# One TensorE-heavy tail and one batch boundary rearranged: a product pair in two sums, three groups parked in SBUF, two sigmoids one block earlier

## The chip, the cores and the metric

The kernel runs on one core of a Trainium2 chip. The metric is device microseconds of one execution; the kernel before takes 492.13 us (median of 3 runs, 490.97 to 493.98). All times below are microseconds from the start of the span of one profiled execution, unless a unit is given.

## The reference, cut to what matters

The input `x` and the side input `k` (used as key and as value) are (4, 1024, 1024): four batches, 1024 rows in time, 1024 channels. A bidirectional decaying scan runs along time, its result is gated by a sigmoid of `x`, and a feed-forward product with a binarized weight follows, with the input added.

```python
ek  = exp(min(k, 30));  ekv = ek * k
nf, df = scan forward  of (ekv, ek):  a = a*decay + ekv_t ; b = b*decay + ek_t
nb, db = scan backward of (ekv, ek)
euk = exp(min(u + k, 30))
num = nf + nb - ekv + euk * k
den = df + db - ek + euk
mix = sigmoid(x) * (num / max(den, 1e-8)) * (0.8 + 0.2*tf)      # tf: one number per batch
bw  = where(weight >= 0, 1, -1) * mean(|weight|, axis=1)        # (out, in)
out = x + einsum('bsi,oi->bso', mix, bw) + bias
```

## The kernel before, in words

**Steps.** Work is cut into blocks of 128 channels by 1024 time steps: 4 batches of 8 blocks, so 32 steps, `g` = 0 to 31. The order of instructions on every engine is written out by hand (`tc.manual_schedule()`); each engine runs its own list in order and waits on semaphores for the others. There is no planner: what stands earlier in the list of an engine blocks what stands later.

**One step on each engine.** SP (the DMA queue of SyncE) loads `k_rows` and `sg_rows` two steps ahead. TensorE (PE) transposes `k_rows` to `kT` (L266) and `sg_rows` to `sgT` (L272), both in PSUM. ScalarE (ACT) takes exponentials of `kT` (L278, L284), a logarithm and an exponential that together are a reciprocal (L404, L411), tiny edge factors for the backward scans (L372, `edge_num` and `edge_den`) and the rounded high part of the gated result (L433, `act_hi`). VectorE (DVE) has eight instructions of 128x1024 in each step: four scans (L366, L379) and four others (L350, L356, L389, L423). GpSimd (POOL) has the floor (L396), a clamp (L346), three products (L416, L419, L428) and the low part of the gated result (L438, `lo_part`), which is stored in `gated` beside the high part. A block that is scanned in step g has its high and low part ready in step g + 2. Sigmoids of two blocks are taken together in every odd step (L111), between two loads of ScalarE's function table (L111 and L94).

**Products of batches 0 to 2.** For each batch there are 16 groups (two halves of time by eight blocks of output channels). A group is a sum of 16 products in PSUM: eight blocks by high and low part (`pe_product`, L449). ACT scales it into SBUF (`z`, L461), PE turns it four times 128x128 (L469), ACT copies it to `staged` (L557), and after two groups SP stores the pair (L135). The lists `parts[g]` and `late[g]` say which pieces of which groups run in which place of a step; `fresh`, `ready`, `scaled`, `leaving` are the stages on the way out. The input `x` is added afterwards in DRAM: `add_x` (L140, POOL's queue) adds 1 MB of `x` into 256 rows of `out` in each call, one call in every second step from step 16 on, and the four calls of batch 2 after step 31.

**The last batch** needs no turning: `pe_wide_product` (L517) uses the gated block as weights, so rows of time come out. There are 8 row groups n by two halves of the columns (`part`), again 16 products each. VectorE multiplies each by `alpha_rows` (L539), adds it to `x_rows[n]` (L541) and adds `bias_rows` (L531); SP stores.

**PSUM** has three buffers in the pool `ps_o`, handed out in turn to `po`, `turned` and `wide` tiles: a new tile waits until the tile three allocations earlier has been read out. `ps_k` and `ps_g` hold `kT` and `sgT` and are used for wide groups at the end.

Of the kernel before, what the change touches and what calls it, by code (L numbers as in the profile page):

```python
# [21 lines left out]
def kernel(  # L22
# [28 lines left out]
    P = 128  # L51
# [8 lines left out]
    const = ctx.enter_context(tc.tile_pool(name="const", bufs=1))  # L60
    gpool = ctx.enter_context(tc.tile_pool(name="gpool", bufs=3 * NC))
    rows = ctx.enter_context(tc.tile_pool(name="rows", bufs=2))
    gate_rows = ctx.enter_context(tc.tile_pool(name="gate_rows", bufs=3))
    resid = ctx.enter_context(tc.tile_pool(name="resid", bufs=2))
# [40 lines left out]
    def load_gate(g):  # L105
        t = gate_rows.tile([P, NT, P], F32, tag="sg_rows", name=f"sg_rows_{g}")
        nc.sync.dma_start(out=t, in_=column_block(x, g))
        sg_rows[g] = t
# [5 lines left out]
    def group(q):  # L114
        b, r = divmod(q, NH * NC)
        h, oc = divmod(r, NC)
        return b, h, oc
# [16 lines left out]
    def store(q):  # L134
        nc.sync.dma_start(out=pair_of(out, q), in_=x_pairs[q])  # L135

    def add_x(b, n):

        rows = slice(2 * n * P, 2 * (n + 1) * P)
        nc.gpsimd.dma_start(  # L140
            out=out[b, rows, :], in_=x[b, rows, :], accum_op=ALU.add, max_dma_last_dim=8192
        )
# [284 lines left out]
    def gated_product(g, ts=slice(0, T), engine=nc.gpsimd):  # L427
        engine.tensor_mul(nums[g][:, ts], dens[g][:, ts], nums[g][:, ts])  # L428
# [12 lines left out]


    def pe_product(q, blocks):
        b, h, oc = group(q)
        if q not in prods:
            prods[q] = ps_o.tile([P, H], F32, tag="po", name=f"po_{q}")
        for cc in blocks:
            for i in range(2):
                nc.tensor.matmul(  # L449
                    prods[q],  # L450
                    wT[:, cc, oc * P : (oc + 1) * P],
                    gated[b, cc, h][:, i, :],
                    start=(cc == 0 and i == 0),
                    stop=(cc == NC - 1 and i == 1),
                )

    def act_scale(q):
        b, h, oc = group(q)
        one = slice(oc, oc + 1)
        z = work.tile([P, H], F32, tag="z", name=f"z_{q}")  # L460
        nc.scalar.activation(  # L461
            z, prods[q], AF.Identity, scale=out_scale[:, b, one], bias=bias_col[:, one]
        )
        z_sb[q] = z
# [47 lines left out]

    def pe_wide_columns(t, n, cols, blocks):
        h, s = divmod(n, PER)
        for cc in blocks:
            for i in range(2):
                nc.tensor.matmul(  # L517
                    t,
                    gated[last, cc, h][:, i, s * P : (s + 1) * P],
                    wT[:, cc, cols],  # L520
                    start=(cc == 0 and i == 0),
                    stop=(cc == NC - 1 and i == 1),
                )
# [5 lines left out]

    def dve_add_bias(n):  # L530
        nc.vector.tensor_add(x_rows[n], x_rows[n], bias_rows)  # L531

    def columns(part):
        return slice(part * H, (part + 1) * H)

    def leave_columns(ps, n, cols):
        width = cols.stop - cols.start
        t = work.tile([P, width], F32, tag="z", name=f"wide_{n}_{cols.start}")
        nc.vector.tensor_mul(t, ps, alpha_rows[:, cols])  # L539
        xs = x_rows[n][:, cols]  # L540
        nc.vector.tensor_add(xs, xs, t)  # L541

    def leave_wide(n, part):
        leave_columns(wide[n, part], n, columns(part))

    def store_wide(n, part):
        rows = out[last, n * P : (n + 1) * P, columns(part)]
        nc.sync.dma_start(out=rows, in_=x_rows[n][:, columns(part)])

    def finish_wide(n):  # L550
        dve_add_bias(n)
        nc.sync.dma_start(out=out[last, n * P : (n + 1) * P, :], in_=x_rows[n])

    def act_leave(q):
        if q % 2 == 0:
            stage(q)
        nc.scalar.copy(x_res[q], turned[q])  # L557
        if q % 2 == 1:
            store(q - 1)

# [11 lines left out]
    def pieces(qs):  # L572
        return [(q, part) for q in qs for part in (front, back)]

    def fill(g, part, items):
        for i, piece in enumerate(items):
            ahead, at = divmod(part + i, 5)
            parts[g + ahead][at].append(piece)
# [9 lines left out]
    for i in range(3):  # L588
        parts[g - 1][2 + i].append((q + i, front))
        parts[g][1 + i].append((q + i, range(NC // 2, NC - 1)))  # L590
        late[g + 1].append((q + i, range(NC - 1, NC)))
    for part, piece in enumerate(pieces((q + 3, q + 4))):
        parts[g + 1][1 + part].append(piece)
    fill(g + 2, 0, pieces(range(q + 5, q + groups)))


    adds = {g: [] for g in range(steps + 1)}
    for b in range(B - 1):
        for n in range(NT // 2):
            adds[min((b + 2) * NC + 2 * n, steps)].append((b, n))  # L600

    with tc.manual_schedule():
# [33 lines left out]
        def product(pieces):  # L636
            for q, blocks in pieces:
                pe_product(q, blocks)
                if blocks[-1] == NC - 1:
                    fresh.append(q)  # L640

# [4 lines left out]
        def scale():  # L646
            while ready:
                scaled.append(ready.pop(0))
                act_scale(scaled[-1])

# [9 lines left out]
        for g in range(steps):  # L660
            b, cc = divmod(g, NC)
            final = g == steps - 1
            if g + 2 < steps:
                load_k(g + 2)
                load_gate(g + 2)
            else:
                load_x_rows(g + 2 - steps, rows, "k_rows")
                load_x_rows(g + 4 - steps, gate_rows, "sg_rows")
# [8 lines left out]
            for i in adds[g]:  # L677
                add_x(*i)
            if final:
                done()  # L680
# [58 lines left out]
            scale()  # L739
            if final:  # L740
                pe_wide_product(0, 1, range(NC - 2))
            product(parts[g][2])
            if g == steps - 2:
                pe_wide_product(1, 0, range(NC - 3))
            if g > 0:
                dve_newton_gate(g - 1)
            if g > 0 and not final:
                gated_product(g - 1)
            gates = (g + 1, g + 2) if cc % 2 == 1 and not final else ()
            if g == 0:  # L750
                gates = (0, 1)
            for i in gates:
                act_gate(i)
            if gates:
                log_exp_tables()
            pe_transpose_gate(g)
            product(parts[g][3])
            turn()
            if parts[g][4]:
                done()  # L760
            product(parts[g][4])
            if g == steps - 2:
                pe_wide_product(1, 1, range(NC - 3))
            if final:
                gate = num_pool.tile([P, T], F32, tag="num", name="gate_of_last")
                nc.scalar.copy(gate, sg_ps[g])
                sg_ps[g] = gate
            leave()
# [10 lines left out]
        load_x_rows(4, gate_rows, "sg_rows")  # L779
        for i in adds[steps]:  # L780
            add_x(*i)

        for i in ((2, 1), (3, 0), (3, 1)):
            pe_wide_product(*i, range(NC - 2))

# [5 lines left out]
        for ts in halves:  # L791
            act_reciprocal(g, ts)
        gated_product(g - 1, engine=nc.vector)
        for h in range(NH):
            act_hi(g - 1, h)
        for h, ts in enumerate(halves):
# [6 lines left out]
            lo_part(g, h, nc.vector)  # L803
        for n in range(5, NT):
            load_x_rows(n, eu_pool, "eu")

        waiting = [(n, part) for n in range(4) for part in range(2)]
        for i in waiting:
            pe_wide_product(*i, range(NC - 2, NC))
        for i in waiting:  # L810
            leave_wide(*i)
        biased = iter((0, 4, 1, 5, 2, 6, 3))
        for n in range(4, NT - 1):
            for part in range(2):
                pe_wide_product(n, part, range(NC))
                if n != 5:
                    leave_wide(n, part)
                    finish_wide(next(biased))

            for part in range(2 if n == 5 else 0):  # L820
                leave_wide(n, part)
                finish_wide(next(biased))
        dve_add_bias(NT - 1)
        finish_wide(next(biased))
        n = NT - 1
        for cols, pool, tag in (
            (slice(0, H), ps_o, "po"),
            (slice(H, 3 * H // 2), ps_o, "po"),
            (slice(3 * H // 2, C), ps_k, "kT"),
        ):  # L830
            bank_of = pool.tile([P, cols.stop - cols.start], F32, tag=tag, name=f"last_{cols.start}")
            pe_wide_columns(bank_of, n, cols, range(NC))
            leave_columns(bank_of, n, cols)
            nc.sync.dma_start(
                out=out[last, n * P : (n + 1) * P, cols], in_=x_rows[n][:, cols]
            )

# [29 lines left out]
```

## Time and profile before

| | |
|---|---|
| time, median of 3 | 492.13 us (490.97 to 493.98) |
| the profiled execution | 494.9 us, of it 493.1 us span |
| DVE busy | 475.5 us, 96% of the span |
| POOL / PE / ACT busy | 402.2 / 369.1 / 336.8 us |
| granted TensorE clock, mean | 0.875 |
| one step on DVE | 13.5 us (num L379 at 380.00, 393.50, 407.10) |
| last scan of DVE | starts at 439.78 |
| last 54 us | PE busy without a gap from 434.76 to 488.93 |

A line of the profile names the engine, the source line, the operation, output and input tiles and the count. In a timeline the columns are start, duration, what ran, and in brackets the idle time of that engine just before it and what ended it. The chain of work that ended last is followed back from the last instruction. Busy time of an engine is no bound by itself: DVE is 96% busy over the span, but in the last 54 us PE has no gap and DVE has.

### The profile page before, as it was taken

The numbers are of one execution on the slowest core, as the hardware profiler recorded it, in microseconds if no ns is written. First come the engines' busy times: TensorE is split into PE (matmuls) and PEld (weight loads), VectorE is DVE, ScalarE is ACT, GpSimd is POOL, SyncE is SP. The second block draws the span as 40 slices with busy tenths as digits, with TensorE's granted clock in tenths as the row PEclk, the third lists the DMA queues.
The fourth block names the chain that finished last, engine by engine and source line by source line (L and its number), as shares of the span: only waits on it lengthen the run. The fifth ranks groups of instructions, "written<-read, shape, count | busy, mean of one in ns | idle before, by whom it ended". The sixth has DMA issues, their size and how long they took to land.

```text
span 493.1 us, 5241 instructions
## 1 busy us (share of the span) xinstructions
PE 369.1 (75%) x1813; PEld 298.4 (61%) x1813; DVE 475.5 (96%) x331; ACT 336.8 (68%) x466; POOL 402.2 (82%) x276
## 2 busy tenths in 40 slices
PE   3334443334677788778999999978699998989996
PEld 2333333233555666666777777756587777868885
DVE  6999999999999999999999999999989999998967
ACT  4795968779585868669696878784597978724000
POOL 3389999999999999999999999999979999991000
PEclk9955555556899999979999999979799999989999
DMA  8846556663546655549976996799389499899945
GB/s 226 231 127 164 142 138 167 170 170 85 144 113 170 159 150 143 142 107 233 255 161 155 266 234 168 147 240 226 75 136 292 99 270 256 193 244 221 255 183 198
DMA packets 89762, 89.49 MB, mean 181 GB/s; under 512 B 2660, under 2 KB 80776, under 8 KB 88200
## 3 DMA queue, kind: packets, MB, share of 16 engines
q1 hardware_dynamic: 83320, 59.78, 40.5%
q0 software_dynamic: 6400, 29.37, 31.5%
q8 instruction: 14, 0.23, 0.2%
q14 instruction: 12, 0.10, 0.1%
q10 hardware_dynamic: 16, 0.00, 0.0%
HBM read 55.59 MB, written 29.36 MB: 172 GB/s over the span
## 4 chain that ended last, share of the span: by engine, by line
DVE 60%; PE 21%; ACT 7%; POOL 6%; issue 4%; DMA 0%; SPq 0%; POOLq 0%; DVEq 0%; ACTq 0%
DVE den L379 11%; DVE num L366 10%; DVE den L366 10%; DVE num L379 9%; PE wide L517 8%; PE po L449 7%; DVE den L389 5%; DVE den L423 5%; DVE num L350 5%; DVE euk L356 3%; POOL den L416 2%; PE last L517 1%; POOL gated L438 1%; PE kT L266 1%; ACT eu L404 1%
## 5 line engine op out<-in xcount | busy, mean ns | idle before, releaser
L449 PE MATMUL po<-gated,wT 128*128 128x512 f32 x768 | 204.7, 413 | 5.4 <-POOL gated L438 3.7
L449 PEld LDWEIGHTS po<-gated,wT 128*128 128x128 f32 x768 | 142.4, 194 | 35.4 <-POOL gated L438 4.0
L266 PE MATMUL kT<-ident,k_rows 128*128 128x128 f32 x248 | 42.6, 328 | 61.6 <-issue 39.0
L438 POOL TENSOR_TENSOR gated<-num,gated 128x512 fp32r<-128x512 f32 x60 | 75.6, 1280 | 5.2 <-ACT gated L433 3.0
L379 DVE TENSOR_TENSOR_SCAN num<-bank,edge_num,num 128x1024 f32<-128x1024 f32 x32 | 74.9, 2339 | 2.7 <-ACT edge_num L372 2.7
L266 PEld LDWEIGHTS kT<-ident,k_rows 128*128 128x128 f32 x248 | 34.1, 168 | 71.0 <-issue 47.3
L379 DVE TENSOR_TENSOR_SCAN den<-bank,edge_den,den 128x1024 f32<-128x1024 f32 x32 | 74.9, 2341 | 1.0 <-ACT edge_den L372 1.0
L416 POOL TENSOR_TENSOR den<-den,eu 128x1024 f32<-128x1024 f32 x31 | 73.7, 2377 | 2.4 <-ACT eu L411 2.4
L419 POOL TENSOR_TENSOR num<-num,eu 128x1024 f32<-128x1024 f32 x31 | 73.7, 2379 | 1.0 <-DMA num<-euk 1.0
L428 POOL TENSOR_TENSOR num<-den,num 128x1024 f32<-128x1024 f32 x30 | 71.9, 2395 | 2.8 <-DVE den L423 0.5
L272 PE MATMUL sgT<-ident,sg_rows 128*128 128x128 f32 x256 | 42.9, 322 | 41.3 <-DVE den L423 36.0
L366 DVE TENSOR_TENSOR_SCAN den<-bank,den 128x1024 f32<-128x1024 f32 x32 | 72.3, 2259 | 0.0
L366 DVE TENSOR_TENSOR_SCAN num<-bank,num 128x1024 f32<-128x1024 f32 x31 | 70.6, 2278 | 0.0
L272 PEld LDWEIGHTS sgT<-ident,sg_rows 128*128 128x128 f32 x256 | 35.1, 166 | 52.7 <-DVE den L423 25.2
L396 POOL TENSOR_SCALAR den<-den,floor 128x1024 f32<-128x1024 f32 x31 | 36.5, 1178 | 21.1 <-DVE den L389 15.7
L433 ACT CAST gated<-num 128x512 fp32r<-128x512 f32 x64 | 36.5, 619 | 22.6 <-POOL num L428 18.2
L557 ACT COPY staged<-turned 128x512 f32<-128x512 f32 x48 | 27.7, 578 | 33.1 <-PE turned L469 33.1
L404 ACT ACTIVATE eu<-den,gain 128x1024 f32<-128x1024 f32 (+1 forms) x33 | 36.9, 1121 | 17.6 <-POOL den L396 17.6
L517 PE MATMUL wide<-wT,gated 128*128 128x512 f32 x192 | 46.6, 400 | 2.1 <-POOL gated L438 2.1
L517 PEld LDWEIGHTS wide<-wT,gated 128*128 128x128 f32 x192 | 36.7, 192 | 10.5 <-POOL gated L438 2.5
L389 DVE SCALAR_TENSOR_TENSOR den<-eu,top,den 128x1024 f32<-128x1024 f32 (+1 forms) x33 | 41.7, 1265 | 0.0
L356 DVE SCALAR_TENSOR_TENSOR euk<-eu,top,kT 128x1024 f32<-128x1024 f32 x31 | 38.8, 1250 | 0.0
(91 smaller groups left out, 579.9 us busy)
## 6 DMA issues: line engine op xcount, KB each, us to landing
sg_rows<-in_x_dram SPq DMA_DIRECT2D x32, 512.0 KB, 5.5
num<-euk POOLq DMA_DIRECT2D x32, 512.0 KB, 5.9
k_rows<-in_fside_BxSxS_dram SPq DMA_DIRECT2D x31, 512.0 KB, 4.9
out_dram<-staged SPq DMA_DIRECT2D x24, 512.0 KB, 4.1
out_dram<-in_x_dram POOLq DMA_DIRECT2D x12, 1024.0 KB, 11.9
w_rows<-in_L_ffn_weight_dram SPq DMA_DIRECT2D x8, 512.0 KB, 5.0
x_rows<-in_x_dram SPq DMA_DIRECT2D x8, 512.0 KB, 12.5
out_dram<-x_rows SPq DMA_DIRECT2D x7, 512.0 KB, 2.6
```

The costliest lines, as they stand in the source:

```text
L266: nc.tensor.transpose(kT[:, s * P : (s + 1) * P], k_rows[g][:, s, :], ident)
L272: nc.tensor.transpose(t[:, s * P : (s + 1) * P], sg_rows[g][:, s, :], ident)
L356: nc.vector.scalar_tensor_tensor(euk, eus[g], top[:, b, cc : cc + 1], k_ps[g], ALU.min, ALU.mult)
L366: nc.vector.tensor_tensor_scan(t, decay_row(g), t, 0.0, ALU.mult, ALU.add)
L379: nc.vector.tensor_tensor_scan(back, decay_row(g), back, inits[g, which], ALU.mult, ALU.add)
L389: nc.vector.scalar_tensor_tensor(dens[g][:, ts], eus[g][:, ts], top[:, b, cc : cc + 1], dens[g][:, ts], ALU.min, ALU.add,)
L416: engine.tensor_mul(dens[g][:, ts], dens[g][:, ts], eus[g][:, ts])
L419: engine.tensor_mul(nums[g][:, ts], nums[g][:, ts], eus[g][:, ts])
L428: engine.tensor_mul(nums[g][:, ts], dens[g][:, ts], nums[g][:, ts])
L438: engine.tensor_sub(t[:, 1, :], nums[g][:, h * H : (h + 1) * H], t[:, 0, :].bitcast(F32))
L449: nc.tensor.matmul(prods[q], wT[:, cc, oc * P : (oc + 1) * P], gated[b, cc, h][:, i, :], start=(cc == 0 and i == 0), stop=(cc == NC - 1 an ...
L517: nc.tensor.matmul(t, gated[last, cc, h][:, i, s * P : (s + 1) * P], wT[:, cc, cols], start=(cc == 0 and i == 0), stop=(cc == NC - 1 and i ...
```

## The change

It has five parts.

1. **Two groups of batch 2 in two sums.** `split` names groups 4 and 5 of batch 2, a pair. Their products over blocks 0 to 5 run in step 23, leave through `z` (a plain copy with scale, without bias), turn, `staged` and a store; their blocks 6 and 7 run in step 25 as a sum of their own, and that pair is added into `out` by an accumulating DMA of 512 KB on POOL's queue (`add_sum`, first step after it without an `add_x`; the built order has it in step 27). Groups 0 to 2 of batch 2, whose first halves ran in step 23, now run in step 24.
2. **Sigmoids of blocks 26 and 27 in step 24** in place of step 25, with their loads earlier (`gate_loads`), `gate_rows` with four buffers and `gpool` with one less.
3. **Three groups of the last batch over five blocks.** In step 30 PE sums groups (6,0), (6,1) and (5,0) over blocks 0 to 4; ACT copies them to SBUF (`act_partial`). The groups (1,0) and (1,1) move behind them. At the end PE has only blocks 5 to 7 of these three groups left. POOL multiplies the parked sums by `alpha_rows` and adds them, with the bias, to `x_rows[6]` and half of `x_rows[5]`.
4. **The end in another order**: row groups 4, 7, 5, 6. Group 4 leaves through an ACT copy and two POOL operations for each half, and is stored from ACT's queue. VectorE multiplies in place in PSUM. Of the four `add_x` of batch 2, one moves to step 29, one stays right behind step 31, two stand behind POOL's work on `x_rows[6]` and `x_rows[5]`. `x_rows` are loaded in the order 5, 7, 6.
5. **The copy of the last gate** stands behind the reciprocals of the last block, and (0,1) behind it; `scale()` holds at most two scaled groups.

The diff, cut to its core:

```diff
-    gpool = ctx.enter_context(tc.tile_pool(name="gpool", bufs=3 * NC))
+    gpool = ctx.enter_context(tc.tile_pool(name="gpool", bufs=3 * NC - 1))
-    gate_rows = ctx.enter_context(tc.tile_pool(name="gate_rows", bufs=3))
+    gate_rows = ctx.enter_context(tc.tile_pool(name="gate_rows", bufs=4))
...
+    split = (2 * NH * NC + 4, 2 * NH * NC + 5)
+    before, after = range(NC - 2), range(NC - 2, NC)
     def pe_product(q, blocks):
+        ends = (0, NC - 1)
+        if q in split:
+            ends = (blocks[0], blocks[-1])
...
     def act_scale(q):
+        if q in split and q not in halved:
+            halved.add(q)
+            nc.scalar.activation(z, prods[q], AF.Copy, scale=out_scale[:, b, one])
...
     def leave_columns(ps, n, cols):
-        t = work.tile([P, width], F32, tag="z", name=f"wide_{n}_{cols.start}")
-        nc.vector.tensor_mul(t, ps, alpha_rows[:, cols])
+        nc.vector.tensor_mul(ps, ps, alpha_rows[:, cols])
         xs = x_rows[n][:, cols]
-        nc.vector.tensor_add(xs, xs, t)
+        nc.vector.tensor_add(xs, xs, ps)
...
+    def add_sum(q):
+        nc.gpsimd.dma_start(out=pair_of(out, q), in_=x_pairs[q], accum_op=ALU.add)
+    def pe_partial(n, part, blocks):
+        if (n, part) not in partial_ps:
+            partial_ps[n, part] = ps_o.tile([P, H], F32, tag="po", name=f"partial_{n}_{part}")
+        pe_wide_columns(partial_ps[n, part], n, columns(part), blocks, (0, NC - 4))
+        return blocks[-1] == NC - 4
+    def act_partial(n, part):
+        if part == 0:
+            partials[n] = resid.tile([P, C], F32, tag="x_res", name=f"partial_{n}")
+        nc.scalar.copy(partials[n][:, columns(part)], partial_ps[n, part])
...
     for i in range(3):
-        parts[g - 1][2 + i].append((q + i, front))
-        parts[g][1 + i].append((q + i, range(NC // 2, NC - 1)))
+        parts[g][1 + i].append((q + i, front))
+        (parts[g][2 + i] if i < 2 else parts[g + 1][0]).append((q + i, range(NC // 2, NC - 1)))
         late[g + 1].append((q + i, range(NC - 1, NC)))
-    for part, piece in enumerate(pieces((q + 3, q + 4))):
-        parts[g + 1][1 + part].append(piece)
-    fill(g + 2, 0, pieces(range(q + 5, q + groups)))
+    parts[g - 1][1].append((split[0], before))
+    parts[g - 1][2].append((split[1], before))
+    fill(g + 1, 1, pieces((q + 3,)) + [(i, after) for i in split])
+    fill(g + 2, 0, pieces(range(q + 6, q + groups)))
+    g = steps - 2
+    parts[g][0].append(("partial", 6, 0, range(NC - 4)))
+    parts[g][1].append(("partial", 6, 0, range(NC - 4, NC - 3)))
+    parts[g][2].append(("partial", 6, 1, range(NC - 3)))
+    parts[g][3].append(("partial", 5, 0, range(NC - 3)))
+    parts[g][4].append(("wide", 1, 0, range(NC - 3)))
+    parts[g + 1][0].append(("wide", 1, 1, range(NC - 3)))
...
+    adds[steps - 3].append(adds[steps].pop(0))
+    gates = {g: (g + 1, g + 2) if g % 2 == 1 and g < steps - 1 else () for g in range(steps)}
+    gates[0] = (0, 1)
+    gate_loads = {g: [g + 2] for g in range(steps)}
+    g = 3 * NC
+    gates[g], gates[g + 1] = gates[g + 1], ()
+    gate_loads[g - 1].extend(gate_loads.pop(g))
+    gate_loads[g], gate_loads[g + 1] = [], []
...
+        for n in (5, 7, 6):
             load_x_rows(n, eu_pool, "eu")
+        for n, cols in ((6, slice(0, C)), (5, slice(0, H))):
+            add_bias(n, nc.gpsimd)
+            t, xs = partials[n][:, cols], x_rows[n][:, cols]
+            nc.gpsimd.tensor_mul(t, t, alpha_rows[:, cols])
+            nc.gpsimd.tensor_add(xs, xs, t)
+        for i in adds[steps]:
+            add_x(*i)
...
+        for part in range(2):
+            pe_wide_product(4, part, range(NC))
+            t = work.tile([P, H], F32, tag="z", name=f"wide_sb_{part}")
+            nc.scalar.copy(t, wide[4, part])
+            nc.gpsimd.tensor_mul(t, t, alpha_rows[:, columns(part)])
+            nc.gpsimd.tensor_add(xs, xs, t)
+        for part in range(2):
+            pe_wide_product(7, part, range(NC))
+            leave_wide(7, part)
+            add_bias(2 + part)
+            store_rows(2 + part)
+        store_rows(4, engine=nc.scalar)
...
+        pe_wide_columns(both[:, 1, :], 5, columns(1), range(NC))
+        pe_wide_columns(both[:, 0, :], 5, columns(0), rest, ends)      # rest: blocks 5 to 7
...
+        for cols in (slice(0, H), slice(H, 3 * H // 2), slice(3 * H // 2, C)):
+            pe_wide_columns(t, 6, cols, rest, ends)
+            leave_columns(t, 6, cols)
+            store_rows(6, cols)
```

## The prediction

> **What bounds the kernel now.** I read the timeline of VectorE first, for waits inside its cadence; then the chain of waits, for what ends the span; then the timelines of TensorE and ScalarE around both places; last the DMA issues. All fences are of the kernel before.
>
> ```profile
> 355.92 2.35 DVE L379 TENSOR_TENSOR_SCAN den<-bank,edge_den,den 128x1024 f32<-128x1024 f32 x1 [0.54 <-ACT edge_den L372]
> 366.06 2.35 DVE L379 TENSOR_TENSOR_SCAN num<-bank,edge_num,num 128x1024 f32<-128x1024 f32 x1 [2.11 <-ACT edge_num L372]
> 370.83 1.22 DVE L423 SCALAR_TENSOR_TENSOR den<-den,sgT 128x1024 f32<-128x1024 f32 x1 [0.24 <-POOL den L416]
> ```
>
> Up to 442 VectorE sets the pace, 13.5 us a step. Behind its first steps and before 442 it stands only at these three places, 2.89 us together, at the border from batch 2 to the last batch, and for 0.8 at the border before (227.5 and 232.3). The two tables and two sigmoids on ScalarE are the cause of the longest:
>
> ```profile
> 358.92 1.28 ACT L111 ACT_TABLE_LOAD   x1
> 360.21 2.01 ACT L111 ACTIVATE sg_rows<-sg_rows 128x1024 f32<-128x1024 f32 x2
> 362.24 1.28 ACT L94 ACT_TABLE_LOAD   x1
> 365.72 0.30 ACT L372 ACTIVATE edge_num<-num,edge 128x1 f32<-128x1 f32 x1
> ```
>
> The edge factor stands behind 4.6 us of table loads and sigmoids. The end belongs to TensorE; in the chain (start, length, what):
>
> ```profile
> 457.82 23.80 PE wide L517 x104
> 481.62 7.30 PE last L517 x48
> ...
> 489.41 0.43 DVE x_rows L541
> ```
>
> 104 products of 512 columns in 23.80 us are 0.2288 each. From 434.76 to 488.93 (54.17 us) TensorE has no gap; VectorE ends 0.91 later, at 489.84, and the last store and the close take 3.26 more.
>
> **Part 1, the border.** Step 24's slot on ScalarE, into which the sigmoids go, has this wait:
>
> ```profile
> 345.41 1.14 ACT L433 CAST gated<-num 128x512 fp32r<-128x512 f32 x2 [4.32 <-POOL num L428]
> ```
>
> The new work there is one staged copy (0.5) and 1.28 + 2.01 + 1.28 of sigmoids: from the edge factor's end at 341.1 to 346.2, or 347.4 if TensorE, cold after standing in step 23, comes late with the turn. The cast begins 0.8 to 2.0 later; the logarithm behind it has 1.24 of idle time before it, and the edge factor behind that is needed at 349.75, by my count between 349.0 and 349.8. So VectorE loses 0 to 0.1 there. The two extra scalings (0.68 each) and turns lie in idle stretches of ScalarE and TensorE in steps 23 and 24 (2.79 of TensorE before 326.76, for one). In step 25 ScalarE keeps three pairs of staged copy and scaling, done near 361.2; the next edge factor can go at 362.9 and is needed at 363.95. I take all 2.89 as gained; the bounds are 0 (the stall only moves to step 24) and 2.89. The load of block 27's gate is issued after step 23's turn of `sg_rows` (about 331) and needed at 343.6, against a median landing of 5.5 for `sg_rows`: hidden, and SP's next load behind it, `k_rows` of block 26, still goes out before its old 337.5. The added 512 KB DMA of step 27 and its issue on POOL (bounded by 0.84 and 1.64, POOL's DMA rows) stand where an even step has its 1 MB one without VectorE waiting: nothing. A staged copy on ScalarE at the end of that step, with the casts behind it, waits for this DMA to land; it is issued some 10 us ahead, against landings of 5.9 (`num<-euk`, 512 KB on the same queue) to 11.9 (1 MB): 0 to 2, I take 0. The 1 MB moved to step 29 sits behind that step's `num<-euk` on POOL's queue, and what waits for the next one, L419, comes 9 us after its issue against landings of 5.0 to 10.2: 0 to 1.0, I take 0.
>
> **Part 2, step 30.** 30 products leave the end (6.86 us) and go to step 30; (1,1) moves to step 31's start. In the built order of the changed kernel the second parked sum takes the PSUM buffer of the first. So it waits for ScalarE's copy of the first, which stands in ScalarE's list behind the edge factor of step 30 and a staged copy:
>
> ```profile
> 425.15 0.30 ACT L372 ACTIVATE edge_den<-den,edge 128x1 f32<-128x1 f32 x1
> 425.35 0.56 ACT L557 COPY staged<-turned 128x512 f32<-128x512 f32 x1
> ```
>
> These are tied to VectorE's scan (425.04) and don't come sooner. The copy is bounded by L557 (0.58) and half of L766's 1.02 for twice the width; with 0.5, TensorE starts the second sum at 426.35, and has stood since 423.6 (last turn at 423.15). Such a wait costs again afterwards:
>
> ```profile
> 326.76 1.11 PE L469 MATMUL turned<-ident,z 128*128 128x128 f32 x4 [2.79 <-ACT z L461]
> 327.53 3.76 PE L449 MATMUL po<-gated,wT 128*128 128x512 f32 x8
> 434.76 1.65 PE L517 MATMUL wide<-wT,gated 128*128 128x512 f32 x3 [2.10 <-POOL gated L438]
> ```
>
> After 2.79 us of idling, a turn, eight products and one transpose of a gate took 5.7 where the usual rows (0.45, 1.83, 0.87) make 3.15: 2.5 lost. After 2.10, three products took 1.44 for 0.69 and those behind them were late too: 1.8 in all. At 350.28, after 3.70, it was 2.9. I take 2.4.
>
> The Trainium skill, "TensorE: Matmul & The Clock Gate", section "What's actually happening", says the array drops to half clock after an idle window of about 3.4 us. By that a wait of 2.8 may cost nothing and the sum below would end at 485.6 in place of 488.0; the two rows above, both shorter than that window, speak for the loss.
>
> From 426.35 TensorE has: 30 products for the second and third parked sum and (1,0), 20 for (1,1) and (2,0), 6 of block 5, 24 for group 0, 12 and 24 for the rest of groups 2 and 3, 32 for blocks 6 and 7 of groups 0 to 3, 32 + 32 for groups 4 and 7, 22 for group 5, 6 for group 6, hence 240 at 0.2288 = 54.91; 12 half-width 1.37; two gate transposes 1.74; the loss 2.4. Sum 60.42: end at 486.77, against 488.93. With the border, 483.88.
>
> What waits for the late third sum: it ends at 426.35 + 2.29 + 0.87 + 2.29 + 2.4 = 434.2 in times of before. Behind its copy (0.5) stand on ScalarE two casts (1.05), the logarithm (1.1) and the edge factor (0.3), and VectorE's backward scan, 434.22 before, waits for that until about 437.2: 3.0. This gives the border's gain back on VectorE, but TensorE doesn't feel it: each tile that it then needs from VectorE, ScalarE or POOL is ready 0.9 to 4 us before its turn. The parked sums lie in buffers of `staged`, so the third copy also waits for the last store of batch 2, issued near 426 and landing in 3.3 to 6.2: before 432.2, hidden by the third sum itself. The gate's copy behind the reciprocals brings VectorE 0.5 of its 1.39 wait at 447, hidden in the same way.
>
> **Part 3, the end.** VectorE's eight leaves at 1.33 (454.89 to 465.51 for eight) and three bias adds at 1.14 end near 469, then it follows TensorE. Multiplying in place in PSUM is a form not shown; L539 (0.68, from PSUM) and L541 (0.69, in SBUF) bound it: I take 0.69, nothing on the path. The last four leaves queue: group 5 second half to 482.5, 512 columns of group 6 to 484.0, two of 256 at 0.92: 485.8, that is 1.9 behind TensorE in place of 0.91. The span then ends at 485.8 + 3.26 = 489.0, 4.1 below 493.1.
>
> POOL takes row groups 6 and 5 and half of the leaving of 4. `x_rows[6]` is loaded last, into a buffer free at about 452. With a landing of 4 POOL works from 456: four of 2.38 and two of 1.28 (12.1), then issues two `add_x` (0.86 each) at 468 to 470:
>
> ```profile
> out_dram<-in_x_dram POOLq DMA_DIRECT2D x12, 1024.0 KB, 11.9
> out_dram<-x_rows SPq DMA_DIRECT2D x7, 512.0 KB, 2.6
> ...
> q0 software_dynamic: 6400, 29.37, 31.5%
> ```
>
> 31.5% of 493.1 for 29.37 MB is 5.3 a MB, so 5.55 for each: 11.1, with five stores (1.35 each by 512 KB at 390 GB/s) beside them: done at 487 or so. This cover is thin, under 2 us.
>
> **The sum.** −2.89 (border) −2.16 (TensorE) +0.95 (leaves at the end) = −4.1: 489.0 of span, 490.8 for the profiled execution in place of 494.9. The median of before is 2.8 below that execution; I take the 4.1 off the median: 488.0.
>
> **The rivals.**
>
> *The wait in step 30 is small.* If TensorE keeps its clock (−2.4) and stands one microsecond for 2.8 (−1.8), the end is 483.8; with the first alone 485.6. For it: in step 30 TensorE has just run 8 products without a break. Against: ScalarE's list is in order, and L372 waits for the scan in every step (17.3 in all). About 485.0.
>
> *The border stays.* The sigmoids push step 24's edge factors as far as they pushed those of step 25: 2.89 back, 490.9. For it: my margin at 349.75 is nearly zero. Against: 4.32 of idle time in that slot, where step 25's sigmoids had none.
>
> *The adds come too late.* In the end of before, the last `x_rows` load took 20.4 from issue to landing, behind four adds. With a landing L, all ends at 452.0 + L + 12.1 + 1.7 + 11.1 + 1.3 = 478.2 + L. From L = 10.8 this sets the end, from 14.9 the gain is gone, and 20.4 makes 498.6, or 497.6 on the median: slower. Against: one add is ahead of that load now, not four.
>
> **How the numbers follow.** Forecast 0.47 (alone 486.5 to 490.5); small wait 0.33; border stays 0.10; late adds 0.10. A measurement of this kernel tells about 1% from no change: below 487.2 is faster, above 497.1 slower. Faster: 0.33 and the low end of the forecast, 0.07: 0.40. Slower: 0.08, since the late adds at moderate L fall within. Same: 0.52. The range takes in the forecast, the border and most of the small wait: 483.5 to 492.5.
>
> **What would show it.** Right: no wait over 0.3 at the three VectorE lines above; sigmoids of step 24 directly ahead of a cast; a TensorE gap of 2 to 3 us before the second parked sum, with slow products after it; a VectorE wait of 1 to 3 for `edge_num` in step 31; the last product about 5 earlier. Wrong: a wait at step 24 or 25, no gap in step 30, or a span that ends with an `add_x` rather than a store of group 6.

## The result, and the profile after

The changed kernel takes 496.08 us (median of 5 runs, 495.47 to 496.88) against 492.13 for the kernel before (now the median of 5 runs, 490.97 to 493.98): ratio 1.0079, 95% interval 1.0058 to 1.0101. It is 0.8% slower, 8.1 us above the forecast and outside its range. The profiled execution took 495.47, of it 493.4 us span.

On VectorE the border went as forecast. In the timeline of VectorE after the change (start, length, what ran, idle time before it) the three waits of before are gone, and a later one is new:

```profile
354.38 2.33 DVE L379 TENSOR_TENSOR_SCAN den<-bank,edge_den,den 128x1024 f32<-128x1024 f32 x1
362.33 2.34 DVE L379 TENSOR_TENSOR_SCAN num<-bank,edge_num,num 128x1024 f32<-128x1024 f32 x1
366.78 1.22 DVE L423 SCALAR_TENSOR_TENSOR den<-den,sgT 128x1024 f32<-128x1024 f32 x1
...
420.70 2.35 DVE L379 TENSOR_TENSOR_SCAN num<-bank,edge_num,num 128x1024 f32<-128x1024 f32 x1 [2.73 <-ACT edge_num L372]
```

No bracket stands at the first three lines. In the timeline of ScalarE the sigmoids of blocks 26 and 27 now lie in step 24, directly ahead of a cast:

```profile
342.12 2.01 ACT L111 ACTIVATE sg_rows<-sg_rows 128x1024 f32<-128x1024 f32 x2
...
345.44 1.14 ACT L433 CAST gated<-num 128x512 fp32r<-128x512 f32 x2
```

The new wait at 420.70 comes from step 29, again by way of ScalarE:

```profile
416.29 1.06 ACT L111 ACTIVATE sg_rows<-sg_rows 128x1024 f32<-128x1024 f32 x1 [3.96 <-DMA sg_rows<-in_x_dram]
...
420.37 0.29 ACT L372 ACTIVATE edge_num<-num,edge 128x1 f32<-128x1 f32 x1
...
426.48 0.62 ACT L589 COPY partial<-partial 128x512 f32<-128x512 f32 x1
```

A sigmoid waited 3.96 for its `sg_rows`. The edge factor stands behind it, and VectorE, which had been 3.65 ahead of the profile of before at its scan of 376.35 (380.00 there), is back at the old time at 420.70 (420.60 there). In the chain of work that ended last the cause is one piece: the load of `sg_rows`, issued at 401.24, took 15.02 to land, one microsecond behind the `add_x` that the change put into step 29 (issued at 400.26). The median for `sg_rows` was 5.5 before. TensorE stood in step 30 as well:

```profile
419.49 0.66 PE L485 MATMUL turned<-ident,z 128*128 128x128 f32 x4 [1.82 <-ACT z L476]
...
422.59 0.49 PE L533 MATMUL partial<-wT,gated 128*128 128x512 f32 x1 [1.33 <-POOL gated L438]
423.61 1.07 PE L485 MATMUL turned<-ident,z 128*128 128x128 f32 x4 [0.52 <-ACT z L476]
424.33 3.83 PE L533 MATMUL partial<-wT,gated 128*128 128x512 f32 x10
```

Three waits, 3.67 together, and then ten products in 3.83 (granted clock 0.61 from 424 to 428) where the next ten take 2.55 at a granted clock of 1.00. None of the three is the one of the forecast: the second parked sum starts at 424.33, and the copy of the first one only at 426.48 (last line of the fence before). TensorE's last products:

```profile
481.06 2.90 PE L533 MATMUL rest<-wT,gated 128*128 128x512 f32 x18
```

They end at 483.96; 483.88 was forecast. But the span does not end 5 sooner than the 493.1 of before. VectorE's end, and then the DMA engines by stretches (the last two columns are the busy share of the 16 DMA engines and GB/s, the one before them the granted clock):

```profile
466.98 6.73 DVE L868 TENSOR_TENSOR x_rows<-x_rows,bias_rows 128x1024 f32<-128x1024 f32 x3
...
486.78 0.42 DVE L552 TENSOR_TENSOR x_rows<-x_rows,rest 128x256 f32<-128x256 f32 x1
```

```profile
465.00:470.00 5.00, 5.00 (x23) 4.10 (x22) 4.93 (x5) 1.18 (x2) 4.92 (x4) 1.00 0.12 49
470.00:475.00 5.00, 5.00 (x24) 4.09 (x23) 4.96 (x5) 0.00 (x0) 4.92 (x5) 1.00 0.98 211
...
485.00:490.00 5.00, 0.00 (x0) 0.00 (x0) 2.14 (x5) 0.00 (x0) 0.00 (x0) 0.86 1.03 419
```

VectorE's last instruction ends at 487.20, the span 6.2 later. From 470 to 490 all 16 DMA engines are busy (0.97 or more in each stretch of 5); from 465 to 470 they are nearly idle. In the list of DMA issues the last figure is the median time from issue to landing:

```profile
out_dram<-x_rows SPq DMA_DIRECT2D x6, 512.0 KB, 7.4
```

A store of 512 KB took 2.6 before by the same median and takes 7.4 here. The two late adds were issued from 469.66 on; everything that is stored at the end shares the DMA engines with them.

### The profile page after: what moved, and what is told of

It reads as the page before. It is cut to its first block, busy times and chain, and to the rows that moved or that the text cites. A ratio compares the mean times of both kernels' runs of the same rounds, so it can differ in the third digit from the quotient of the medians.

```text
span 493.4 us, 5238 instructions
## 1 busy us (share of the span) xinstructions
PE 368.1 (75%) x1811; PEld 298.0 (60%) x1811; DVE 475.4 (96%) x325; ACT 341.8 (69%) x475; POOL 423.7 (86%) x287
## 4 chain that ended last, share of the span: by engine, by line
DVE 62%; PE 17%; POOL 8%; issue 5%; DMA 3%; ACT 3%; SPq 0%; POOLq 0%; DVEq 0%; ACTq 0%
DVE den L379 11%; DVE den L366 10%; DVE num L379 10%; DVE num L366 10%; PE wide L533 8%; DVE den L389 5%; DVE den L423 5%; DVE num L350 5%; PE po L457 3%; DMA sg_rows<-in_x_dram 3%; DVE euk L356 3%; POOL den L416 2%; POOL gated L438 2%; POOL num L428 1%; PE partial L533 1%
## 5 line engine op out<-in xcount | busy, mean ns | idle before, releaser
L419 POOL TENSOR_TENSOR num<-num,eu 128x1024 f32<-128x1024 f32 x31 | 74.1, 2391 | 0.0
L396 POOL TENSOR_SCALAR den<-den,floor 128x1024 f32<-128x1024 f32 x31 | 38.5, 1243 | 19.9 <-DVE den L389 16.3
L563 ACT COPY staged<-turned 128x512 f32<-128x512 f32 x50 | 28.9, 577 | 32.5 <-PE turned L485 32.3
L533 PE MATMUL wide<-wT,gated 128*128 128x512 f32 x182 | 42.7, 392 | 0.0
L533 PEld LDWEIGHTS wide<-wT,gated 128*128 128x128 f32 x182 | 34.1, 188 | 7.4
```

The costliest lines, as they stand in the source:

```text
L419: engine.tensor_mul(nums[g][:, ts], nums[g][:, ts], eus[g][:, ts])
L533: nc.tensor.matmul(t, gated[last, cc, h][:, i, s * P : (s + 1) * P], wT[:, cc, cols], start=(cc == ends[0] and i == 0), stop=(cc == ends[1 ...
```

## The experiments

Each comparison has its own runs of the kernel before beside it (medians 492.06 to 492.4); a difference below is against those. The changed kernel stands at +3.95.

**1. Without the two late adds.** Their 512 rows of batch 2 then lack `x`.

```diff
-        for i in adds[steps]:
-            add_x(*i)
```

> The changed kernel without the two add_x that stand behind POOL's work on row groups 6 and 5 (512 rows of batch 2 come out without x). Theory Q: the end is set by the DMA queue, busy from 469.5 to 491.7 with two adds of 1 MB and the stores, while VectorE ends at 487.2. Then the span ends about 3.3 behind VectorE's last operation, near 490.5 in place of 493.4, and the time falls by about 3, to 493. The last stores land in 2 to 3 us in place of 5 to 8. Theory V: the end is set by VectorE, whose bias adds took 2.24 each beside POOL in place of 1.22; then leaving the adds out changes nothing: 496.

491.66, 0.63 below before (ratio 0.9986, interval 0.9972 to 1.0000). The span ends 3.2 behind VectorE's last instruction (486.7), in place of 6.2. That is 4.6 better than the changed kernel, where Q expected about 3 and V nothing. So the late adds hold the end; what VectorE does there is hidden behind them.

**2. The same adds sooner**, right behind POOL's first bias addition.

```diff
         for n, cols in ((6, slice(0, C)), (5, slice(0, H))):
             add_bias(n, nc.gpsimd)
+            if n == 6:
+                for i in adds[steps]:
+                    add_x(*i)
...
-        for i in adds[steps]:
-            add_x(*i)
```

> The changed kernel with the two late add_x issued behind the first POOL operation on row group 6 (about 459) in place of behind the sixth (469.7): the DMA engines stood idle from about 460 to 469. Theory Q: the adds are through by about 471, the last stores find an empty queue, span near 490.5, time near 493. Theory V: no gain, or 1 to 2 lost because POOL issues before it multiplies: 496 to 498.

492.89, +0.60 (1.0013, 1.0001 to 1.0025): 3.35 better than the changed kernel with the same work. The same stretches:

```profile
460.00:465.00 5.00, 5.00 (x23) 4.09 (x23) 4.86 (x8) 0.16 (x1) 4.92 (x4) 1.00 1.03 205
...
475.00:480.00 5.00, 5.00 (x24) 4.09 (x23) 4.96 (x4) 0.00 (x0) 3.96 (x3) 1.00 0.28 113
```

The DMA engines are full from 460 to 470 with the adds (2 MB, some 11 us) and mostly idle from 475 to 480 (share 0.28), before the last stores come. VectorE's last instruction ends at 487.1, as in the changed kernel, so VectorE was not what the changed kernel's end hung on.

**3. The moved add in step 31** instead of step 29.

```diff
-    adds[steps - 3].append(adds[steps].pop(0))
+    adds[steps - 1].append(adds[steps].pop(0))
```

> The changed kernel with the first add_x of batch 2 in step 31 in place of step 29. Theory S: this 1 MB beside the loads of step 29 makes sg_rows of block 31 land 15 after its issue in place of 5.5, ScalarE's sigmoid waits 4.0 for it, and VectorE 2.73 for edge_num; in step 31 no load is urgent, so VectorE's wait at 418 falls below 0.5 and the last scan starts near 437.5 in place of 440.1. Rival: the load is late from the backlog of step 28's add; then the wait stays. For the time: if the end hangs on the DMA queue (theory Q), it moves by less than 1; if it hangs on VectorE's chain, it falls by 2.5.

494.13, +1.84 (1.0035, 1.0017 to 1.0054): 2.1 better. The wait at 420.70 is gone, the last scan starts at 437.47 (440.14 in the changed kernel), TensorE's last group at 477.82 (481.06). The span still ends 7.0 behind VectorE, at the DMA engines. I had expected less than 1 of gain in that case and had overlooked that the late adds hang on the same chain: they are issued at 467.70 here, 1.96 sooner.

**4. The border alone**: the kernel before, with the pair in two sums and the sigmoids in step 24 (parts 1 and 2 of the change, with the limit of two scaled groups in `scale()`), and nothing of the tail.

```diff
+    parts[g - 1][1].append((split[0], before))
+    parts[g - 1][2].append((split[1], before))
+    fill(g + 1, 1, pieces((q + 3,)) + [(i, after) for i in split])
+    gates[g], gates[g + 1] = gates[g + 1], ()
```

> The kernel before with the border alone: the pair in two sums and the two sigmoids in step 24, with their loads; the end of before. If the border's 2.89 of VectorE waits are gone and reach the end: VectorE's last scan starts near 436.9 in place of 439.8, time 489.2 to 490 in place of 492.1. Rival: they only move to step 24 or 25, or TensorE at the end takes them back: 491.5 to 493.

492.11, −0.18 (0.9988, 0.9977 to 0.9999). Yet VectorE's last scan starts at 437.09, 2.69 before that of the profile of before (439.78). Either the gain was lost behind 437, or the profile of before was late.

**5. The kernel before, profiled again, twice.** No edit.

> The kernel before, unchanged, profiled a second time. The border alone made the last scan start 2.7 sooner than in the profile of before (437.09 against 439.78), yet its median is 0.2 below that of before. Theory H: the profile of before caught a late execution (span 493.1, where most executions of before have spans near 490.5), and the stall of 2.1 at the edge factor of step 25 and the others of the border are smaller or absent in an ordinary one. H expects a span near 490.5, the last scan near 437.3, and less than 1 of waits at the three lines of the border. Rival P: the waits of 2.9 are there in every execution, the last scan starts near 439.8 again, and TensorE's end is what varies: then the border is worth 2.9 on VectorE and something later gives it back.

> The kernel before, unchanged, profiled once more, for the scatter of what the run with it shows: by H the waits of the border vary between executions (sum under 1 in an ordinary one, up to 2.9 in a late one) and the last scan varies with them; by P they are 2.9 in all of them.

The first has a span of 490.2, the second 492.4. Of 23 executions of before in one comparison 19 have spans from 489.2 to 490.8 and four from 492.1 to 493.6; the profile that I worked from, with 493.1, is one of the late kind. In the ordinary one VectorE waits less at the border:

```profile
364.44 2.35 DVE L379 TENSOR_TENSOR_SCAN num<-bank,edge_num,num 128x1024 f32<-128x1024 f32 x1 [1.14 <-ACT edge_num L372]
```

1.14 in place of 2.11, and 0.54 and 0.24 at the other two: 1.92, not 2.89. H had the span right (490.5 expected), but both theories missed the waits: they are in all three profiles, and one of them varies (2.12 in the third). What varies behind it is TensorE's clock. From 352 to 356 the granted clock is 0.50 in the profile of before and 0.83 in the ordinary execution; ten products that delay the turn and then ScalarE take 3.87 and 2.89. It is the clock at such a place that counts, as only a profile shows it: the mean clock of an execution does not tell the two kinds apart (0.875 to 0.886 or 0.975 in late ones, 0.881 to 0.989 in ordinary ones). At 433 the same happens again, first in the ordinary execution, then in the third profile, which is a late one:

```profile
433.13 0.97 PE L517 MATMUL wide<-wT,gated 128*128 128x512 f32 x3 [2.10 <-POOL gated L438]
```

```profile
433.79 1.65 PE L517 MATMUL wide<-wT,gated 128*128 128x512 f32 x3 [2.10 <-POOL gated L438]
```

After the same idle time of 2.10, three products take 0.97 or 1.65. The granted clock from 435 to 438 is 1.00 in the ordinary execution and 0.50 in the profile of before. TensorE's ends in these two are 3.1 apart: 0.64 from the first steps, 0.97 from the border and some 1.5 from here. The Trainium skill, "TensorE: Matmul & The Clock Gate", "What's actually happening", says that the activity window runs freely, so that the moment of a change depends on where in the window the work falls: the scatter agrees with that. Its length of some 3.4 us of idling before the clock drops does not: here 2.10 is enough in two executions of three.

Against the ordinary execution the border alone has its last scan 1.06 sooner, and TensorE's last part 0.43 later, by the timeline of TensorE with the border alone:

```profile
432.07 1.65 PE L531 MATMUL wide<-wT,gated 128*128 128x512 f32 x3 [2.47 <-POOL gated L438]
```

It stands 2.47 in place of 2.10, and the clock drops (0.50 from 432 to 434). VectorE loses its gain a little later: its first operation behind the scans of the last block starts at 444.36 in both executions, after 1.50 of waiting for ScalarE with the border and 0.49 without.

**6. The border alone, with the gap filled.** Eight products with a weight of zeros are added to an open sum.

```diff
+                for _ in range(8):
+                    nc.tensor.matmul(wide[1, 0], zeros, wT[:, 0, :H], start=False, stop=False)
                 for i in ((1, 0), (1, 1), (2, 0)):
                     pe_wide_product(*i, range(NC - 3, NC - 2))
```

> The border alone, and in step 31, ahead of the products of block 5 where TensorE stood 2.47 for POOL and then ran three products in 1.65 in place of 0.69, eight products with a weight of zeros are added into the open sum (1.83 of work in a gap of 2.47). Theory W: the border's gain on VectorE (last scan 1.06 sooner than in the second profile of before) is lost because TensorE comes to that gap sooner, stands longer and runs at half clock for 3 us after it, which costs 1.5. Without the gap it expects a granted clock of 1.00 between 432 and 438, TensorE's last product 1.5 sooner than with the border alone, and a time of 490.4 to 490.9 against 492.1. Rival R: the end does not hang on TensorE's pace there, and the time stays at 492.0 to 492.3.

491.96, −0.44 (0.9982, 0.9967 to 0.9998): no gain beyond that of the border. The clock did what theory W said. It is 1.00 from 432 to 439, and TensorE turns the last gate at 438.74, against 440.34 with the border alone:

```profile
431.75 1.20 PE L533 MATMUL wide<-wT,gated 128*128 128x512 f32 x4
...
478.48 7.59 PE L533 MATMUL last<-wT,gated 128*128 128x512 f32 x48
```

But the last part starts at 478.48 against 478.75. The stall has only moved; VectorE now waits for the block's own numerator, which comes by DMA on POOL's queue:

```profile
445.75 0.69 DVE L421 TENSOR_TENSOR num<-num,eu 128x512 f32<-128x512 f32 x1 [1.88 <-DMA num<-euk]
```

So W is right on the clock and wrong on the time, and R holds: the end does not hang on TensorE's pace there. TensorE's lead over the border alone is 1.60 at 438.74 and 0.27 at 478.48; its only waits in between are 0.16 and 0.26, both for VectorE. That the wait of 1.88 is what takes the lead is a reading of this profile and not shown: no run removes it.

**7. Both cures**: the edits of 2 and 3 together.

> The changed kernel with both cures: the late adds issued right behind the first bias addition of POOL, and the add of step 29 in step 31. Theory Q (the late adds and eight stores share the DMA queues at the end) with S (the load of sg_rows is delayed by the add of step 29): both gone, so the end is VectorE's: its last instruction near 484.7 as with the add in step 31, 2.7 to 3.3 behind it the end of the span, 487.4 to 488.0, and 489.3 to 490.0 of time: 0.5% below before. Rival D (the queues just have too much to move from 450 on, wherever the adds stand): span 489.5 or more, no better than 491.5, since the add of step 31 now meets the loads of x_rows and the two late adds.

491.03, −1.03 (0.9981, 0.9962 to 1.0000): 4.98 better than the changed kernel, where the two alone brought 3.35 and 2.11. Neither theory had the time: Q with S expected 489.3 to 490.0, D 491.5 or more. The span ends 3.2 behind VectorE's last instruction, as in run 1 without the late adds, so the DMA engines no longer set it. VectorE and TensorE at the end:

```profile
464.00 7.36 DVE L868 TENSOR_TENSOR x_rows<-x_rows,bias_rows 128x1024 f32<-128x1024 f32 x3
...
485.15 0.42 DVE L552 TENSOR_TENSOR x_rows<-x_rows,rest 128x256 f32<-128x256 f32 x1
```

```profile
477.44 2.94 PE L533 MATMUL rest<-wT,gated 128*128 128x512 f32 x18
```

TensorE ends at 480.38, VectorE at 485.57, 5.2 behind it. Three bias additions take 7.36 that take 3.5 in the kernel before, where POOL has nothing to do at the end. The changed kernel shows both prices in one execution, with the DMA engines full all the while (1.01 from 475 to 480): an addition beside POOL takes 2.24, and the two right behind POOL's last instruction, which ends at 478.37, take 2.35 together.

```profile
474.96 2.24 DVE L868 TENSOR_TENSOR x_rows<-x_rows,bias_rows 128x1024 f32<-128x1024 f32 x1
478.46 2.35 DVE L868 TENSOR_TENSOR x_rows<-x_rows,bias_rows 128x1024 f32<-128x1024 f32 x2
```

**8. Additions sorted by where their inputs lie.** POOL takes the bias of groups 0 to 3 (both inputs in SBUF), VectorE the leaving of group 4 (one input in PSUM), and the halves of group 5 get PSUM tiles of their own.

```diff
-        for i in (0, 4, 1):
-            add_bias(i)
...
+        add_bias(4)
+        for part in range(2):
+            pe_wide_product(4, part, range(NC))
+            leave_wide(4, part)
+        for i in range(4):
+            add_bias(i, nc.gpsimd)
```

> As the run with both cures, and at the end all additions from SBUF to SBUF go to POOL where it can take them (the bias of groups 0 to 3), all that come from PSUM to VectorE (group 4 too); the two halves of group 5 lie in PSUM tiles of their own. Theory C: VectorE and POOL slow each other when both add from SBUF (bias additions 2.2 on VectorE beside POOL against 1.2 without), and this makes VectorE the bound of the end. C expects VectorE to have waits for TensorE from 475 on, TensorE's last product near 480.7, VectorE's last instruction 1.2 to 2 behind it at 482 to 482.7, a span of 485 to 486, and a time of 487 to 488.0. Rival: the end hangs on the stores in the queues, and the time is that of the run with both cures, 489.3 or more.

490.38, −1.68 (0.9968, 0.9954 to 0.9982). VectorE has the waits for TensorE that C expected (1.37 and 0.68 near the end) and ends 1.7 behind it (484.45 against 482.75), where it was 5.2 in run 7. With run 7 this shows that the bias additions beside POOL held VectorE back. But the time missed C's 488 by 2.4. The profile is of the slowest of this run's 12 executions (span 490.8, the others 487.5 to 488.9), so its times are some 2 late: in it POOL ended its four additions (10.50) at 482.58, and stores stood behind them in SP's queue.

**9. Three stores on ScalarE's queue**, and the bias of group 3 back on VectorE.

```diff
-        for i in range(4):
+        for i in range(3):
             add_bias(i, nc.gpsimd)
+        add_bias(3)
...
+        for i in range(3):
+            store_rows(i, engine=nc.scalar)
```

> As the run with the additions sorted by where their inputs lie, but POOL takes the bias of groups 0 to 2 only, VectorE that of group 3 in its wait ahead of group 7, and the stores of 0 to 2 go by ScalarE's queue, so that no store of SP's queue stands behind POOL. Theory: in that run the last store landed 6 behind VectorE's last instruction, because POOL ended its four bias additions at 482.6 and the stores behind them in SP's queue came in a bunch. It expects 3.2 between VectorE's last instruction and the span's end, a span of 485.5 to 486.5 and a time of 487.6 to 488.6. Rival: the bytes themselves keep the queues busy (eight stores of 512 KB, 1.35 each, from 474 on), and the time stays at 490.0 to 490.5.

489.81, −2.59 (0.9951, 0.9931 to 0.9971): the fastest here by its median, faster than both kernels. The two edits are not told apart. The end is 3.2 behind VectorE, as expected; VectorE itself is 4.1 behind TensorE (484.58 against 480.51), which was not, and the time is 1.2 above the 488.6 expected at most. One addition from SBUF to SBUF beside POOL, and behind it an instruction with one input in PSUM:

```profile
469.73 3.39 DVE L868 TENSOR_TENSOR x_rows<-x_rows,bias_rows 128x1024 f32<-128x1024 f32 x1
473.04 0.69 DVE L550 TENSOR_TENSOR wide<-wide,alpha_rows 128x512 f32<-128x512 f32 x1
```

3.39 where POOL is busy with 2.4 to 2.7 of its own, 0.69 for the other at the same time.

**10. The same, with the add behind step 31 moved** to the other two.

```diff
-        add_x(*adds[steps].pop(0))
```

> As the run with a queue of their own for three stores, and the add that stood right behind step 31 goes with the other two, behind POOL's first bias addition: all three are issued near 457. Theory: in that run VectorE waited 1.88 at 446 for the block's own numerator on its way by DMA (issued near 436, the add at 439 shares the queues with it), and VectorE has no idle time behind it until its last instruction at 484.6, while TensorE, without a gap from 445, ends 4 sooner. It expects the wait of 1.9 to fall under 0.5, VectorE's end near 483, and a time of 488.0 to 488.7 against 489.8. Rival: three adds from 457 on (5.5 of all queues each) run into the first stores at 472, as in the changed kernel: no better than 489.8, 490.5 or more if the last add lands behind 476.

489.89, −2.23 (0.9945, 0.9924 to 0.9966): no different, as the rival had it. The wait for the own numerator is 1.63 in place of 1.88, so this add was not its main cause. What makes this transfer land 10 us after its issue stays open; the loads of `x_rows` that share the queues with it were not moved.

**11. The tail alone**: as 7, without the border (and without what came with it: the buffers, the limit in `scale()`, the extra turn).

```diff
-    split = (2 * NH * NC + 4, 2 * NH * NC + 5)
+    split = ()
...
-    gates[g], gates[g + 1] = gates[g + 1], ()
```

> The run with both cures without the border: no pair in two sums and the sigmoids in step 25 as before; parts 3 to 5 with the adds mended. Theory A (the parts add up along VectorE): the border's waits of 1.9 in an ordinary execution are back, less 0.5 for the two small ones that the border leaves in step 27, so 1.4 over the run with both cures: 492.4, level with before, and the last scan near 438.5. Rival N (the border is worth what it brings alone, 0.1 at most): 491.0 to 491.3.

501.86, +9.46 (1.0190, 1.0167 to 1.0212). Both theories fell. ScalarE's copy of the third parked sum waits for a buffer of `staged`, and this for the last store of batch 2. ScalarE's timeline, then the chain:

```profile
442.07 0.59 ACT L589 COPY partial<-partial 128x512 f32<-128x512 f32 x1 [11.25 <-DMA out_dram<-staged]
```

```profile
430.36 11.61 DMA out_dram<-staged
```

VectorE's scan behind it waits 10.36. With the border SP sends the last pair at 423.00 (run 7), four microseconds ahead of the `add_x` of step 31; without it the store goes out at 430.36, one behind that `add_x` (429.33), and takes 11.61 to land, against 3.4 in run 7. That the add in front of it is what delays it fits, but was not tried by itself. So the border's worth is not in its own waits: alone it brings next to nothing, but it clears the way for the parked sums and the mended add. The tail without the border and with the add in step 29 was not run.

## Why the prediction was wrong

**The border** (taken as −2.89): the mechanism held, the sigmoids fit into step 24. The size came from a late execution. An ordinary one has 1.92 of waits, and about 0.5 of new ones come in step 27 (0.33 at 376.35). Alone it is worth 0.2 to the time: the gain meets TensorE's gap in step 31 (run 4), and with the gap filled another wait stands behind it (run 6). I also took the gain, worked out on that late execution, off the median, which is of the ordinary kind.

**The add moved to step 29** (0 to 1.0, taken as 0): it cost 2.1 (run 3). Against the ordinary execution of before, VectorE was 2.04 ahead at 376.35 and 1.71 behind at 420.70. I looked only at POOL's own queue and at L419 behind it. The 1 MB shares the 16 DMA engines with SP's loads, and `sg_rows`, which sigmoids wait for in each odd step, was issued one microsecond behind it and took 15.0. In run 3 the same load, issued at 401.72, is read by ScalarE at 412.2 without a wait.

**Step 30** (a wait of 2.8 for the copy and 2.4 of lost clock): that wait does not exist. The prediction had the second sum in the first one's PSUM buffer, behind ScalarE's copy; it started 2.15 ahead of that copy (424.33 and 426.48), so it had another buffer. With the add out of step 29 TensorE stands 1.17 in three pieces there and keeps its clock (run 7). This is the rival of the small wait, which I put at 0.33. That TensorE ended where I said is no proof of my steps: 3.67 of other waits took the place of the wait that I had counted.

**TensorE as a whole**: with both cures it ends at 480.38, against 485.77 in the ordinary execution of before: −5.39, where my sum had −5.05. So what the change was to take from TensorE it does take; by subtraction some 4 of it come from step 30 and the end, and the rest from the border; no run measures the two by themselves.

**VectorE's leaves at the end** (+0.95, 1.9 behind TensorE): 5.2 behind it, 3.3 more, in run 7. I priced the bias additions at 1.14, from the end of before, where POOL is idle; beside POOL's work they take 2.2 to 3.4. The Trainium skill, "SBUF — State Buffer", section "Who interferes with whom", says that a VectorE instruction with two SBUF inputs contends with a GpSimd instruction that reads SBUF, over shared ports that it calls an exclusive lock, and that VectorE with at most one SBUF input, outside its two-port modes, does not. The changed kernel and run 9 agree: 2.24 and 3.39 for the first kind, 0.69 for the second. VectorE's wait for `edge_num` in step 31, which I forecast as 1 to 3, did not come: it followed from the late third sum.

**The late adds** (cover under 2, done at 487 or so, "with five stores beside them"): this step cost the most, 3.35. The landing L was 4.5, so the rival's condition (above 10.8) was not met, and the adds were issued at 469.66, close to the 468 to 470 forecast. But only the first store had been issued by then (468.58). All eight, 1.35 each, share the DMA engines with 11.1 of adds: 469.7 + 11.1 + 10.8 = 491.6, and the engines run empty near 491.5. I counted five in the text, and one (1.3) in the rival's formula; with eight it reads 487.7 + L, which passes the forecast's 489.0 from L = 1.3 on. The sign that I had named, a span that ends with an `add_x`, did not come: the adds landed 11.3 after their issue, near 482, and the stores that they had held up ended the span.

**The account**: −4.1 forecast, +3.95 measured, 8.1 apart. The two adds are 5.0 (run 7), VectorE's end behind TensorE 3.3; the rest, −0.3, is TensorE's.

## What to carry to other kernels

A transfer that is moved is to be checked against every queue that shares the DMA engines with it, not against its own queue alone: add up all bytes of the last stretch, and look for the load that an engine waits for within 15 us. Price an instruction from rows where the other engines do what they will be doing then. Before a stall of one or two microseconds is taken as a gain, a second profile of the same kernel shows whether it is there in every execution.

## What the runs showed of the hardware

- Two 1 MB adds from DRAM to DRAM keep all 16 DMA engines busy for some 11 us (run 2), and what is issued close behind an add lands late: `sg_rows` after 15.0 (median before 5.5), a 512 KB store after 11.6 (3.4 in run 7, where it goes out ahead of the add).
- The granted clock of TensorE fell to 0.50 after 2.10 us of idling in two executions of the same kernel and stayed at 1.00 in a third; between the ordinary and the third profile that makes 0.7 on the next three products and 1.5 by the transposes behind the next 26.
- VectorE's 128x1024 addition from SBUF to SBUF takes 1.22 alone and 2.2 to 3.4 beside POOL's additions and products, while its 128x512 instructions with one input in PSUM stay at 0.69.
